# Summing attention values over slots: two strided reductions a tile instead of pairwise additions

## The chip, the cores and the metric

The kernel runs on one core of a Trainium2 chip. The time is that of one execution on the device, in microseconds (us). The engines have these names in the profile: PE is TensorE (matrix multiplications), PEld its weight loads, DVE is VectorE, ACT is ScalarE, POOL is GpSimd, SP is SyncE. Each engine works through its own instructions in order, and waits for the others through semaphores.

## The reference

The computation is a graph network on 6250 nodes with features of 128 numbers and some 206,000 edges. A first layer spreads features along the edges five times, and a layer norm follows. The second layer is an attention over the edges that arrive at a node:

```
q = (node_attr @ Wq).reshape(n, H, DQ // H)
k = conv(x[src], edge_attr, edge_sh, ..k).reshape(e, H, DK // H)
v = conv(x[src], edge_attr, edge_sh, ..v).reshape(e, H, DV // H)
alpha = einsum('ehq,qk,ehk->eh', q[dst], Wdot, k)
ealpha = exp(alpha - amax[dst])
attn = ealpha / denom[dst]
out = segment_sum(attn[..., None] * v, dst)
return out.reshape(n, DV) @ Wout
```

Here `conv` is `((x_src * (edge_sh @ Wang.T)) @ Wlin) * (relu(edge_attr @ W1 + b1) @ W2)`. There are H = 8 heads; a key has 64 numbers and a value 128, so 16 per head. A last layer norm follows. The change concerns the sum in `out`: for each node, its edges' weighted values are added up.

## The kernel before

The kernel has three stages: it counts edges between nodes in matrices (to about 600 us), it multiplies features with these matrices five times (to about 2140 us), and then comes the attention (`attend`, L859 to L1121), to the end. The first two stages aren't touched.

For the attention, nodes are sorted by their number of edges and put in 49 tiles of 128 nodes, one node per partition. Tile t has `WIDTHS[t]` slots, from 64 to 22, and 1658 in all; a slot holds one edge of every node of the tile. Four slots make a group (the last group of a tile may have fewer), and the loop at L1097 goes over the groups of all tiles as one pipeline, a few groups deep. For a group:

- `fetch` (L914), three groups ahead: POOL issues one indirect DMA per slot (L932), which gathers the features of the edges' source nodes into `xs`, of which there are six buffers.
- `turn` (L956): PE transposes `xs` into PSUM (L961), ACT copies it to `xT` (L964).
- `nets` (L966): PE computes `p_h` and `p_g` from the edge features (L975), ACT applies relu (L977), and DVE multiplies `p_g` with `xT` into `mkv` by two operations (L983). `p_g` has one buffer, so PE's next `nets` waits for this.
- `radial` (L987), one group later: PE computes `p_r` (L994), ACT copies it to `rr` (L998).
- `keys` (L1000): PE computes keys and values in `p_k` (L1008, L1010); `p_k` has one buffer. DVE multiplies them with `rr` into `kv` (L1015), which also frees `p_k`, and then forms the scores `al` (L1017, L1019).

When all groups of a tile are done, `softmax(t)` (L1022) is started. It is a generator, and it goes on to its next `yield` whenever the loop calls `step(running)`: once after `nets` of a group and once after `radial` and `turn` (L1103 and L1108), so twice a group, beside the groups of the next tile. The order of PE, DVE and ACT is this order of the program (`manual_schedule`, L1096). POOL's gathers stand in its own queue in the order of `fetch`.

The steps of `softmax` are: (1) mask, maximum and difference of the scores (L1030 to L1032); (2) exp on ACT (L1034); (3) mask again, denominator, reciprocal (L1036 to L1040); then, for each eight slots, a multiplication of the values with the weights in place (L1046), and from the second eight on an addition onto the first eight (L1050), each a step of its own; then one step with three additions of 4, 2 and 1 slots (L1053); then the division `o` (L1057), a transpose on PE (L1060) and the output product, the residual and the statistics (L1065 to L1067). After tiles 13, 26, 39, 46, 48 and 49 the finished rows are normalised (L1077) and POOL scatters them to the output (L1081), one indirect DMA per tile.

`kv` of a tile is an array of [128, w, 192] floats: per slot 64 numbers of the key and behind them 128 of the value. Neighbouring slots are thus 192 x 4 = 768 bytes apart. Two such arrays exist, used by turns.

Of the kernel before, what the change touches and what calls it, by code (L numbers as in the profile page):

```python
# [7 lines left out]
F32 = mybir.dt.float32  # L8
# [5 lines left out]
OP = mybir.AluOpType  # L14
AX = mybir.AxisListType
# [3 lines left out]
P = 128  # L19
# [12 lines left out]
H = 8  # L32
DK = 64
D = 128
# [174 lines left out]
def stats(nc, work, z, v):  # L209
    st = work.tile([P, nc.vector.BN_STATS_DIM], F32, name="st")  # L210
    nc.vector.bn_stats(st, z)
    nc.vector.bn_aggr(v, st)
# [646 lines left out]
def attend(tc, w1, b1, wang, w2, wlin, wqd, wout, ident, rows, c_iota, src_all, eas_o, x1_d, x1_r, out):  # L859


    nc = tc.nc
    WM = WIDTHS[0]
    with ExitStack() as s:
        one = s.enter_context(tc.tile_pool(name="at1", bufs=1))
        two = s.enter_context(tc.tile_pool(name="at2", bufs=2))
# [12 lines left out]
        with tc.tile_pool(name="at_w", bufs=1) as pool:  # L879
            wz = pool.tile([P, 2 * D], F32, name="wz")  # L880
            nc.vector.memset(wz, 0.0)
            for src, dst, at in ((w1, w1_s, 0), (wang, wang_s, 64)):
                n = src.shape[1]
                nc.vector.tensor_copy(dst, wz[:, :n])
                w = pool.tile([16, n], F32, name=f"w_{at}")
# [20 lines left out]
        def ps(name):  # L906
            return pp.tile([P, CH], F32, name=name, tag="ps")
# [114 lines left out]
        def softmax(t):  # L1022

            w = WIDTHS[t]
            a = kv[t]
            l = al.pop(t)[:, :w]
            ex = two.tile([P, WM, H], F32, name="ex")
            m = two.tile([P, H], F32, name="m")
            d = two.tile([P, H], F32, name="d")
            nc.vector.tensor_tensor(l, l, keep[t][:, :w, None].to_broadcast([P, w, H]), OP.min)  # L1030
            nc.vector.tensor_reduce(m, l.rearrange("p j h -> p h j"), AX.X, OP.max)
            nc.vector.tensor_tensor(l, l, m[:, None, :].to_broadcast([P, w, H]), OP.subtract)  # L1032
            yield
            nc.scalar.activation(ex[:, :w], l, AF.Exp)  # L1034
            yield
            nc.vector.tensor_tensor(ex[:, :w], ex[:, :w],  # L1036
                                    ok[t][:, :w, None].to_broadcast([P, w, H]), OP.mult)
            nc.vector.tensor_reduce(d, ex[:, :w].rearrange("p j h -> p h j"), AX.X, OP.add)
            nc.vector.tensor_scalar(d, d, none[:, t:t + 1], None, OP.add)
            nc.vector.reciprocal(d, d)  # L1040
            yield

            for u in range(0, w, 8):
                k = min(8, w - u)
                av = a[:, u:u + k, DK:].rearrange("p j (h f) -> p j h f", h=H)
                nc.vector.tensor_tensor(av, av, ex[:, u:u + k, :, None].to_broadcast([P, k, H, D // H]),  # L1046
                                        OP.mult)
                yield
                if u > 0:
                    nc.vector.tensor_add(a[:, :k, DK:], a[:, :k, DK:], a[:, u:u + k, DK:])  # L1050
                    yield
            for h in (4, 2, 1):
                nc.vector.tensor_add(a[:, :h, DK:], a[:, :h, DK:], a[:, h:2 * h, DK:])  # L1053
            yield
            av = a[:, :1, DK:].rearrange("p j (h f) -> p j h f", h=H)
            o = two.tile([P, H, D // H], F32, name="o")
            nc.vector.tensor_tensor(o, av[:, 0], d[:, :, None].to_broadcast([P, H, D // H]), OP.mult)  # L1057
            yield
            tr = ps("tr4")
            nc.tensor.transpose(tr[:, :P], o.rearrange("p h d -> p (h d)"), ident)  # L1060
            oT = two.tile([P, P], F32, name="oT")
            nc.scalar.copy(oT, tr[:, :P])
            yield
            y = ps("y4")
            nc.tensor.matmul(y[:, :D], oT, wo, start=True, stop=True)  # L1065
            nc.vector.tensor_add(z[:, t, :], x1s.pop(t), y[:, :D])
            stats(nc, two, z[:, t, :], v[:, t, :])  # L1067
            if t + 1 in NORMS:
                yield
                t0 = NORMS[NORMS.index(t + 1) - 1]  # L1070
                rs = two.tile([P, NT], F32, name="rs")
                n = t + 1 - t0
                nc.vector.tensor_scalar(rs[:, :n], v[:, t0:t + 1, 1], EPS, None, OP.add)
                nc.scalar.activation(rs[:, :n], rs[:, :n], AF.Sqrt)
                nc.vector.reciprocal(rs[:, :n], rs[:, :n])
                for u in range(t0, t + 1):
                    nc.vector.tensor_scalar(z[:, u, :], z[:, u, :], v[:, u, 0:1],  # L1077
                                            rs[:, u - t0:u - t0 + 1], OP.subtract, OP.mult)

                    k = min(P, N - u * P)  # L1080
                    st = nc.gpsimd.indirect_dma_start(  # L1081
                        out=out[:, :], in_=z[:k, u, :], in_offset=None,
                        out_offset=bass.IndirectOffsetOnAxis(ap=rows[:k, u, 0:1], axis=0)).ins
                    for q in puts:
                        tc.declare_no_dep(st, q, reason="a node has one place in the order")
                    puts.append(st)
                    if u % 4 == 3:
                        yield
# [7 lines left out]
        with tc.manual_schedule(engines=MANUAL):  # L1096
            for i in range(-3, len(groups) + 1):  # L1097
                live = [0 <= i + x < len(groups) for x in range(-1, 4)]
                if live[4]:
                    fetch(i + 3)  # L1100
                if live[1]:
                    nets(i)
                step(running)  # L1103
                if live[0]:
                    radial(i - 1)
                if live[2]:
                    turn(i + 1)
                step(running)  # L1108
                if live[0]:
                    keys(i - 1)  # L1110
                    t, j, n = groups[i - 1]
                    if j + n == WIDTHS[t]:
                        running.append(softmax(t))
                if len(running) > 1:
                    step(running)
                if live[3] and groups[i + 2][1] == 0:
                    begun.append(begin(groups[i + 2][0]))
                step(begun)
            for r in running:
                for _ in r:  # L1120
                    pass  # L1121
# [351 lines left out]
```

## Time and profile before

| | us |
|---|---|
| median of 10 runs | 4434.86 (4428.51 to 4440.15) |
| the profiled execution | 4440.44 |
| its span, first to last instruction | 4438.7 |
| first to last gather of the attention (L932) | 2142.8 to 4385.8 |
| DVE busy, whole span | 3615.9 |
| PE busy, whole span | 3721.4 |
| POOL busy, whole span | 2437.9 |

In a row of a group of instructions stand its line, engine, operation, written and read tiles with their shapes (partitions x elements), the number of instructions, their busy time in us, the mean of one in ns, and the idle time of the engine just before them with what ended it. A row on one line's instructions gives the shortest, median and longest duration in ns and the first and last start. A row of a timeline gives the start, the length, the engine and line, and in brackets the idle time before it and what ended that.

### The profile page before, as it was taken

The numbers are of one execution on the slowest core, as the hardware profiler recorded it, in microseconds if no ns is written. First come the engines' busy times: TensorE is split into PE (matmuls) and PEld (weight loads), VectorE is DVE, ScalarE is ACT, GpSimd is POOL, SyncE is SP. The second block draws the span as 40 slices with busy tenths as digits, with TensorE's granted clock in tenths as the row PEclk, the third lists the DMA queues.
The fourth block names the chain that finished last, engine by engine and source line by source line (L and its number), as shares of the span: only waits on it lengthen the run. The fifth ranks groups of instructions, "written<-read, shape, count | busy, mean of one in ns | idle before, by whom it ended". The sixth has DMA issues, their size and how long they took to land.

```text
span 4438.7 us, 70265 instructions
## 1 busy us (share of the span) xinstructions
PE 3721.4 (84%) x23256; PEld 3306.8 (75%) x23256; DVE 3615.9 (81%) x6081; ACT 2060.2 (46%) x4185; POOL 2437.9 (55%) x2388
## 2 busy tenths in 40 slices
PE   2555569979999999999588998878898878888885
PEld 2555558868888888887587888868888778887785
DVE  4999978657777878665488888879888978899796
ACT  1666665445564665643243433434443434344343
POOL 4233100653333443022677777777777777777774
PEclk9667679989999999999899999989999999999997
DMA  3555345668777888654555555545555655555541
GB/s 109 156 160 161 86 124 141 161 174 236 232 225 219 235 241 239 185 159 132 110 98 101 100 99 106 100 95 103 100 100 96 112 98 99 99 100 103 98 98 44
DMA packets 393183, 603.04 MB, mean 136 GB/s; under 512 B 122942, under 2 KB 328054, under 8 KB 381931
## 3 DMA queue, kind: packets, MB, share of 16 engines
q1 hardware_dynamic: 260352, 361.35, 33.2%
q0 software_dynamic: 128624, 207.89, 20.9%
q10 hardware_dynamic: 3834, 29.20, 2.1%
q8 instruction: 189, 3.10, 0.3%
q14 instruction: 184, 1.50, 0.1%
HBM read 493.45 MB, written 132.25 MB: 141 GB/s over the span
## 4 chain that ended last, share of the span: by engine, by line
PE 45%; DVE 16%; issue 11%; DMA 10%; POOL 10%; SPq 6%; ACT 1%; DVEq 0%; ACTq 0%; POOLq 0%
PE acc L588 23%; DMA xs<-x_d,src_all 7%; PE p_r L994 6%; POOL xs L932 6%; SPq L364 6%; PE p_k L1010 6%; PE p_k L1008 4%; DVE mkv L983 3%; DVE kv L1015 3%; PE p_g L975 2%; DVE oh_h L218 2%; PE p_x L961 2%; DVE oh_l L218 2%; DMA c<-counts 1%; POOL rows_d L747 1%
## 5 line engine op out<-in xcount | busy, mean ns | idle before, releaser
L932 POOL DMA_INDIRECT xs<-x_d,src_all x1658 | 1675.6, 1011 | 506.8 <-issue 432.1
L588 PE MATMUL acc<-c,parts 128*128 128x512 f32 (+1 forms) x6370 | 1412.6, 382 | 55.0 <-DVE c L571 40.7
L588 PEld LDWEIGHTS acc<-c,parts 128*128 128x128 f32 x6370 | 1155.4, 189 | 282.5 <-DVE c L571 47.1
L571 DVE CAST c<-c 128x1024 fp32r<-128x1024 uint8 x980 | 682.3, 714 | 258.0 <-PE acc L588 192.9
L1010 PE MATMUL p_k<-wlin_s,mkv 128*128 128x128 f32 x3316 | 760.2, 312 | 0.0
L584 ACT CAST c<-c 128x512 fp32r<-128x512 uint8 x735 | 454.9, 622 | 561.5 <-PE acc L588 430.8
L1008 PE MATMUL p_k<-wlin_s,mkv 128*128 128x64 f32 x3316 | 585.0, 260 | 65.2 <-DVE kv L1015 64.4
L994 PE MATMUL p_r<-w_s,r 128*128 128x192 f32 x3316 | 621.8, 330 | 0.0
L994 PEld LDWEIGHTS p_r<-w_s,r 128*128 128x128 f32 x3316 | 573.2, 194 | 34.8 <-ACT rr L998 0.2
L1008 PEld LDWEIGHTS p_k<-wlin_s,mkv 128*128 128x128 f32 x3316 | 528.0, 200 | 94.4 <-DVE kv L1015 93.3
L1015 DVE TENSOR_TENSOR kv<-rr,p_k 128x768 f32<-128x768 f32 (+2 forms) x443 | 396.7, 897 | 209.1 <-PE p_k L1010 192.6
L998 ACT COPY rr<-p_r 128x768 f32<-128x768 f32 (+2 forms) x443 | 334.8, 758 | 479.7 <-PE p_r L994 464.1
L983 DVE TENSOR_TENSOR mkv<-p_g,xT 128x512 f32<-128x512 f32 (+3 forms) x866 | 533.8, 658 | 6.6 <-PE p_g L975 6.5
L1010 PEld LDWEIGHTS p_k<-wlin_s,mkv 128*128 128x128 f32 x3316 | 527.8, 201 | 0.0
L977 ACT ACTIVATE r<-p_h,b_s 128x512 f32<-128x512 f32 (+3 forms) x433 | 289.8, 669 | 463.2 <-PE p_h L975 456.3
L812 POOL DMA_DIRECT2D eas_o<-eT_l x252 | 203.1, 809 | 507.8 <-DVE eT_l L806 499.7
L342 PE MATMUL p_c<-oh_h,oh_l 128*128 128x100 bf16 x3136 | 301.9, 273 | 169.4 <-DVE oh_h L218 168.4
L342 PEld LDWEIGHTS <-oh_l 128*128 128x128 bf16 x3136 | 290.3, 123 | 177.6 <-DVE oh_h L218 176.0
L961 PE MATMUL p_x<-ident,xs 128*128 128x128 f32 x1658 | 278.6, 280 | 128.2 <-DMA xs<-x_d,src_all 121.3
L961 PEld LDWEIGHTS p_x<-ident,xs 128*128 128x128 f32 x1658 | 212.8, 142 | 161.2 <-DMA xs<-x_d,src_all 127.8
L344 ACT CAST cT<-p_c 128x500 uint8<-128x500 f32 (+1 forms) x637 | 306.3, 638 | 47.1 <-DVE c_row L350 46.9
L964 ACT COPY xT<-p_x 128x512 f32<-128x512 f32 (+3 forms) x433 | 247.9, 573 | 136.1 <-PE p_x L961 132.0
(215 smaller groups left out, 4338.0 us busy)
## 6 DMA issues: line engine op xcount, KB each, us to landing
c<-counts SPq DMA_DIRECT2D x360, 384.0 KB
ea<-eas_o SPq DMA_DIRECT2D x648, 128.0 KB
c<-counts SPq DMA_DIRECT2D x120, 448.0 KB
eas_o<-eT_l POOLq DMA_DIRECT2D x162, 256.0 KB
counts<-c_row SPq DMA_DIRECT2D x582, 48.0 KB
xs<-x_d,src_all POOLq DMA_INDIRECT x1658
eat<-in_eas ACTq DMA_DIRECT2D x31, 832.0 KB
counts<-c_row SPq DMA_DIRECT2D x194, 56.0 KB
```

Of the source, the lines that this page charges most:

```text
L342: nc.tensor.matmul(p_c[:, q - q0], oh_los[t % 2][:, q // Q, :, q % Q], oh_hi[:, q // Q, :, q % Q], start=True, stop=True)
L571: nc.vector.tensor_copy(c[:, u:u + 1024].rearrange("p (n b x) -> p n b x", n=2, b=2), r[:, :, v:v + 512].rearrange("p b (n x) -> p n b x", ...
L584: nc.scalar.copy(c[:, 1024:w].rearrange("p (b x) -> p b x", b=2), r[:, :, 512:])
L588: nc.tensor.matmul(a[:, :v - u], parts[:, j, i, :], c[:, u:v], start=(j == 0 and i == 0), stop=(j == NT - 1 and i == 1))
L932: nc.gpsimd.indirect_dma_start(out=xs[g][:, i, :], out_offset=None, in_=x1_d[:, :], in_offset=bass.IndirectOffsetOnAxis(ap=src_all[:, c:c ...
L961: nc.tensor.transpose(p_x[:, i * P:(i + 1) * P], xs[g][:, i, :], ident)
L983: nc.vector.tensor_tensor(mkv[g][:, i, :n].rearrange("p j (b e) -> p b j e", b=4), p_g[:, i, :n * P].rearrange("p (b j e) -> p b j e", b=4 ...
L994: nc.tensor.matmul(p_r[:, i // 2, u:u + DK + D], r[:, i, :], w2_s, start=True, stop=True)
L998: nc.scalar.copy(r2[:, b, :f], p_r[:, b, :f])
L1008: nc.tensor.matmul(p_k[:, i // 2, u:u + DK], m[:, 0, i, :], wlin_s[:, :DK], start=True, stop=True)
L1010: nc.tensor.matmul(p_k[:, i // 2, u + DK:u + DK + D], m[:, 1, i, :], wlin_s[:, DK:], start=True, stop=True)
L1015: nc.vector.tensor_mul(k.rearrange("p (b i) f -> p b (i f)", b=b.stop - b.start), r2[:, b, :f], p_k[:, b, :f])
```

## The change

The multiplications stay as they are, one for each eight slots and each a step. The additions between them and the three additions behind them go. In their place come two reductions with an addition, one for the first four heads and one for the other four, each a step. One reduction reads, for each of 64 value columns, the w slots of the tile, and writes 64 sums into a new small tile `s`. The division then reads `s`.

```diff
                 nc.vector.tensor_tensor(av, av, ex[:, u:u + k, :, None].to_broadcast([P, k, H, D // H]),
                                         OP.mult)
                 yield
-                if u > 0:
-                    nc.vector.tensor_add(a[:, :k, DK:], a[:, :k, DK:], a[:, u:u + k, DK:])
-                    yield
-            for h in (4, 2, 1):
-                nc.vector.tensor_add(a[:, :h, DK:], a[:, :h, DK:], a[:, h:2 * h, DK:])
-            yield
-            av = a[:, :1, DK:].rearrange("p j (h f) -> p j h f", h=H)
+            s = two.tile([P, H, D // H], F32, name="s")
+            for h in range(0, H, 4):
+                f = DK + h * (D // H)
+                nc.vector.tensor_reduce(s[:, h:h + 4].rearrange("p h f -> p (h f)"),
+                                        a[:, :w, f:f + D // 2].rearrange("p j f -> p f j"), AX.X, OP.add)
+                yield
             o = two.tile([P, H, D // H], F32, name="o")
-            nc.vector.tensor_tensor(o, av[:, 0], d[:, :, None].to_broadcast([P, H, D // H]), OP.mult)
+            nc.vector.tensor_tensor(o, s, d[:, :, None].to_broadcast([P, H, D // H]), OP.mult)
```

## The prediction
> **What bounds the kernel now.** I read the page, then the groups of VectorE (DVE) from 2130 us on (the attention stage), the rows of single lines, and one tile's timeline.
>
> ```profile
> span 4438.7 us, 70265 instructions
> ...
> L932 POOL DMA_INDIRECT xs<-x_d,src_all x1658 | 1675.6, 1011 | 506.8 <-issue 432.1
> ```
> ```profile
> L932 POOL DMA_INDIRECT xs<-x_d,src_all x1658: 948/955/2015, 2142.8 to 4385.8; - x185
> ```
> The gathers alone set the pace of this stage: 1675.6 + 506.8 = 2182 us, plus about 65 us of output scatters, fill the 2243 us between the first and the last gather. POOL's idle time is "issue", about 0.3 us a gather. But its lead over DVE and TensorE (PE) is small:
>
> ```profile
> PE p_x L961 <- DMA xs<-x_d,src_all: 121.3, 80, 8.3
> PE p_k L1008 <- DVE kv L1015: 62.2, 98, 1.7
> PE tr L1060 <- DVE o L1057: 43.2, 43, 2.9
> ```
> These are PE's waits in the stage (total, times, longest). Only 121 of 2243 us are waits for gathers: DVE and PE would need some 2120 us without them. Next, what the change touches:
>
> ```profile
> L1050 DVE TENSOR_TENSOR kv<-kv 128x1024 f32<-128x1024 f32 (+7 forms) x180 | 197.2, 1096 | 5.9
> L1053 DVE TENSOR_TENSOR kv<-kv 128x512 f32<-128x512 f32 x147 | 68.8, 468 | 3.5
> ```
> ```profile
> L1031 DVE TENSOR_REDUCE m<-al x49: 470/645/1126, 2247.0 to 4408.2; 128x8 f32<-128x272 f32 x4, 128x8 f32<-128x296 f32 x3, 128x8 f32<-128x288 f32 x3, 128x8 f32<-128x280 f32 x3
> ...
> L1347 DVE TENSOR_REDUCE nviol<-viol x1: 1831/1831/1831, 25.5 to 25.5; 128x1 f32<-128x1612 f32 x1
> ```
> And how the work interlocks, in a tile of 36 slots:
>
> ```profile
> 3007.16 1.28 DVE L983 TENSOR_TENSOR mkv<-p_g,xT 128x512 f32<-128x512 f32 x2
> 3008.36 1.22 DVE L1046 TENSOR_TENSOR kv<-kv,ex 128x1024 f32<-128x1024 f32 x1
> 3009.61 1.22 DVE L1050 TENSOR_TENSOR kv<-kv 128x1024 f32<-128x1024 f32 x1
> 3010.75 0.95 DVE L1015 TENSOR_TENSOR kv<-rr,p_k 128x768 f32<-128x768 f32 x1
> 3011.75 0.43 PE L1008 MATMUL p_k<-wlin_s,mkv 128*128 128x64 f32 x2 [0.72 <-DVE kv L1015]
> 3012.53 1.28 DVE L983 TENSOR_TENSOR mkv<-p_g,xT 128x512 f32<-128x512 f32 x2
> ...
> 3028.74 1.47 DVE L1053 TENSOR_TENSOR kv<-kv 128x512 f32<-128x512 f32 x3
> 3030.24 0.29 DVE L1057 TENSOR_TENSOR o<-kv,d 128x128 f32<-128x128 f32 x1
> 3030.68 0.30 PE L1060 MATMUL tr<-ident,o 128*128 128x128 f32 x1 [0.98 <-DVE o L1057]
> ```
> A group of four slots costs DVE 2.97 us without softmax work (5.36 between starts of mkv, less the two operations' 2.39). PE needs 4.22 us a group (in the light groups p_h at L975 starts at 3040.13 and 3044.34). So softmax work beyond 1.25 us in a group makes DVE the limit, and PE then waits at the p_k bank that L1015 frees.
>
> **The change, part by part.** *Removed:* 180 additions (L1050) and 147 (L1053): 197.2 + 68.8 = 266 us of DVE.
>
> *Added:* 98 reductions of 64 x w elements (w slots in the tile, 1658 in all). Each output value is read along slots, 768 bytes apart. The trace has no such stride; two rows bound it. Contiguous (L1347): 1831 ns for 1612 elements, and L1019's 420 against 220 ns for 256 against 64: 1.04 ns an element. At a step of 32 bytes (L1031: 470 ns at w = 22, 176 elements; 1126 ns at w = 64, 512 elements): 656 / 336 = 1.95 ns an element and 0.126 us fixed. Both are the same operation, so the step between reads makes the difference, and I take 1.95, the scattered one being nearer. 2 x 64 x 1658 = 212,224 elements give 414 us, and 98 x 0.126 us give 12: 426 us. Net: +160 us of DVE. At 1.04 it is 221 + 12 = 233: net -33. Upward no row limits it; a step as large again would add another (1.95 - 1.04) x 212 = 193 us.
>
> The Trainium skill ("VectorE: DVE Perf Modes", section on the perf-mode tier table) puts tensor_reduce at one element a cycle whatever the type. At its 0.96 GHz that is 221 us, as with the contiguous row, and by it the change would save DVE time. The row L1031 says otherwise for scattered reads, and the sum goes by the row.
>
> *Where it lies.* A reduction of the 36-slot tile is one DVE instruction of 64 x 36 x 1.95 + 126 = 4.62 us. Behind it on DVE's queue stand L1015, which frees p_k for PE, and the next mkv, which frees p_g. Softmax steps come two to a group; the first reduction is step 4 + ceil(w/8). With ceil(w/8) odd (w of 33 to 40, and 24 and 22: 23 tiles) both fall into one group, with it even they fall into neighbouring groups (26 tiles).
>
> The 36-slot tile before, between starts of mkv: 5.72, 5.37, 5.36, 5.36, 4.30, 5.28, 5.00, 4.43, 4.55 = 45.4 us. After: 5.72 (unchanged); 5.36 (two multiplications); 2.97 + 1.22 + 0.68 = 4.9 (the last two); 2.97 + 2 x 4.62 + 0.1 = 12.3 (both reductions); then PE's transpose stands before its keys and waits for o, so DVE does mkv and o (1.6), waits 1.9 for the keys, and does the rest (1.8): 5.3; then 4.6, 4.4, 4.3, 4.55. Sum 51.4: +6 us, of which 3.5 is added DVE work and the rest is that early groups were freed of additions they could partly hide. I take 5.8 at the class's mean width of 34.7: 23 x 5.8 = 133.
>
> Split case, w = 30 (a reduction is 3.87 us): the groups 5.57 (mask, denominator, a multiplication), 5.36, 5.36, 2.97 + 2 x 0.95 = 4.87, 4.9 (the three additions, o), 5.0 (transpose) = 31.1 become 5.57, 5.36, 2.97 + 0.95 + 3.87 = 7.8, 2.97 + 3.87 + 0.29 = 7.1, 4.6 (transpose), 4.3 = 34.8. That is +3.7; the DVE work alone is +2.9, and as PE still has one group ahead at the first reduction I take +3: 20 x 3 = 60. Five tiles of 41 to 46 slots, with reductions of 5.2 to 5.9 us, at 4.5, and the 64-slot tile, with 8.1 us, at 10: 32. Together 133 + 60 + 32 = +225 us for DVE and PE.
>
> *What hides part of it.* The gathers go on during a reduction; six buffers of xs let POOL run ahead. So PE's 121 us of waits for gathers go first: 225 - 121 = +104. No more can hide, since POOL's pace no longer decides.
>
> *What comes back.* PE will stand still for up to 10 us a tile (both reductions, L1015, mkv, o, less what it has ahead). The trace shows the price of idling:
>
> ```profile
> 3579.80 0.45 PE L961 MATMUL p_x<-ident,xs 128*128 128x128 f32 x1 [8.25 <-DMA xs<-x_d,src_all]
> ```
> ```profile
> 3575.00:3588.70 13.70, 6.80 (x26) 5.66 (x27) 2.41 (x5) 1.36 (x3) 10.35 (x12) 0.50 0.18 48
> 3588.70:3598.00 9.30, 8.36 (x62) 7.68 (x61) 5.93 (x15) 3.65 (x7) 7.17 (x8) 1.00 0.31 80
> ```
> (The second view: stretch, length, busy time of PE, its weight loads, DVE, ACT and POOL, then granted clock, DMA share, GB/s.) After 8.25 us of idling the granted clock (0.50, then 1.00) is half for some 9 us of resumed work; after idle stretches of 2 us (as at 3103.65) it is half for 3.4 or 6.8 us (the trace's record of the clock). Each reduction stall will cost such a stretch: 1.7 to 3.4 us of PE time while PE is the limit. I take the low end, as some lies beside DVE work: 49 x 1.7 = 83.
>
> *Gathers.* Their mean is 1011 ns against a least of 948, so contention costs at most 0.063 x 1658 = 104 us, and the additions are about a third of the time of DVE's operations with two operands in SBUF (266 of some 760 us, L1046 with 253 and L1017 with 180 the others): some 35 us of POOL time. The Trainium skill ("SBUF — State Buffer", section on who interferes with whom) says that such an operation blocks a GpSimd instruction reading SBUF, and a reduction never does. By it the change would free POOL, which no run here shows. Those 35 us are worth nothing once POOL does not set the pace, so I take 0.
>
> Sum: 225 - 121 + 83 = +187 us on the profiled execution's 4440.44 us, which stands 5.6 us above the median 4434.86: 4434.9 + 187 = 4622 us.
>
> **The rivals.** *A, POOL still hides it.* The stalls would have to fit into what gathers run ahead. For: POOL never shows a wait for a buffer over 0.3 us, and PE mostly reaches a tile's first gather 7 to 18 us after its issue (by the timeline). Against: a buffer moves a stall, and the 36-slot tile's 51.4 us exceeds POOL's 46. Time 4430 to 4480; it needs a sum of 150 us or less where I have 225.
> *B, faster.* If the 768-byte step is read at 1.04 ns an element, a reduction takes 2.5 us, DVE loses 33 us of work, POOL stays the limit, and fewer two-operand operations shorten gathers by up to 35 us: 4400 to 4430. It decides below about 1.1 ns. Against it stands L1031.
> *C, dearer reads.* If 768 bytes costs a step more than 32 bytes, another 193 us, hidden by nothing: some 4820.
>
> **How the numbers follow.** My case 0.74 (own range 4530 to 4780: from no clock loss at 4434.9 + 104 to about half of the waits kept with the clock at 3.4 us), A 0.09, B 0.08, C 0.09. The range runs 4450 to 4790: my case with its bounds and most of A. This kernel can be told from no change at about 0.2% (9 us). Faster 0.08 (B), same 0.04 (half of A), slower 0.88.
>
> **What would show it.** Two reductions a tile near 4.3 us at w = 34, 426 us in all; DVE's idle time lower; PE's wait at L1008 for L1015 in stretches of several us; the wait for xs nearly gone, and gathers waiting over 0.3 us for p_x; half-clock stretches at each tile. It is wrong if a reduction takes 2.4 us (then B), if PE's stalls stay below 3 us a tile (then A), or if the half clock does not follow them (then some 4540).

## The result, and the profile after

The changed kernel takes 4651.2 us (median of 8; 4645.7 to 4655.7) where the kernel before took 4435.0 us (median of 28): a ratio of 1.0486, with a 95% interval of 1.0477 to 1.0495. That is 216 us slower; 187 were forecast. First the head of the page, of the kernel before and then of the changed kernel (busy time, share of the span and number of instructions of each engine):

```profile
PE 3721.4 (84%) x23256; PEld 3306.8 (75%) x23256; DVE 3615.9 (81%) x6081; ACT 2060.2 (46%) x4185; POOL 2437.9 (55%) x2388
```
```profile
span 4648.9 us, 70024 instructions
...
PE 3805.5 (82%) x23256; PEld 3394.2 (73%) x23256; DVE 3723.1 (80%) x5852; ACT 2060.5 (44%) x4185; POOL 2401.7 (52%) x2388
...
L932 POOL DMA_INDIRECT xs<-x_d,src_all x1658 | 1640.3, 989 | 732.2 <-issue 435.0 <-PE p_x L961 245.3 <-DMA xs<-x_d,src_all 19.9
```
PE's line keeps the books of the whole change. It has the same 23256 instructions, but is busy for 84 us more: it ran more of them at half clock (the mean granted clock of the whole run fell from 0.926 to 0.892). And it is idle for 4648.9 - 3805.5 = 843 us in place of 4438.7 - 3721.4 = 717: 126 us more. Both together are the 210 us by which the span grew. POOL, which before waited for PE's L961 to free a buffer of xs for 20 us in all and never over 0.3 us at a time, now waits 245 us for it, up to 9.1 us at a time: its gathers no longer set the pace.

Next, what PE waited for from the start of the attention stage to the end of the kernel (total us, times, longest), in the kernel before and then in the changed kernel:

```profile
PE p_x L961 <- DMA xs<-x_d,src_all: 121.3, 80, 8.3
PE p_k L1008 <- DVE kv L1015: 64.4, 99, 2.1
PE tr L1060 <- DVE o L1057: 57.0, 45, 12.3
PE y L1065 <- ACT xT L964: 38.9, 43, 0.9
```
```profile
PE tr L1059 <- DVE o L1056: 257.9, 49, 14.5
PE p_k L1008 <- DVE kv L1015: 119.6, 110, 6.5
...
PE y L1064 <- ACT xT L964: 19.5, 25, 0.9
...
PE p_x L961 <- DMA xs<-x_d,src_all: 7.7, 8, 2.5
```
So the waits for DVE grew by 256 us, those for gathers fell by 114, and those of the product y by 19: +123 of the 126 us. The longest wait for o, 14.5 us, is that of the last tile, and was 12.3 before.

The reductions, by form, and one tile of 36 slots in the order of time:

```profile
L1052 DVE TENSOR_REDUCE s<-kv 128x64 f32<-128x1408 f32 x2 | 4.9, 2500 | 0.0
...
L1052 DVE TENSOR_REDUCE s<-kv 128x64 f32<-128x2304 f32 x6 | 24.1, 4053 | 0.0
...
L1052 DVE TENSOR_REDUCE s<-kv 128x64 f32<-128x4096 f32 x2 | 14.1, 7052 | 0.0
```
```profile
3087.38 0.33 PE L1008 MATMUL p_k<-wlin_s,mkv 128*128 128x64 f32 x2
...
3087.61 1.28 DVE L983 TENSOR_TENSOR mkv<-p_g,xT 128x512 f32<-128x512 f32 x2
3088.80 8.03 DVE L1052 TENSOR_REDUCE s<-kv 128x64 f32<-128x2304 f32 x2
3096.75 0.94 DVE L1015 TENSOR_TENSOR kv<-rr,p_k 128x768 f32<-128x768 f32 x1
...
3099.78 0.28 DVE L1056 TENSOR_TENSOR o<-s,d 128x128 f32<-128x128 f32 x1
...
3100.20 0.45 PE L1059 MATMUL tr<-ident,o 128*128 128x128 f32 x1 [8.73 <-DVE o L1056]
...
3100.44 0.53 PE L1008 MATMUL p_k<-wlin_s,mkv 128*128 128x64 f32 x2
...
3104.17 0.95 DVE L1015 TENSOR_TENSOR kv<-rr,p_k 128x768 f32<-128x768 f32 x1 [4.12 <-PE p_k L1010]
```
The two reductions hold DVE for 8 us. Behind them stand L1015, the next group's mkv and o, and PE's transpose waits for that o: 8.73 us without work. PE then comes back at half clock (0.53 us for the pair at L1008, in place of 0.33 ahead of the stall), and DVE in turn waits 4.12 us for the keys. At full clock it would still wait some 2.3 us, as `warm2` below shows.

### The profile page after: what moved, and what is told of

Same layout as the page of the kernel before. It is cut to its first block, busy times and chain, and to the rows that moved or that the text cites. A ratio compares the mean times of both kernels' runs of the same rounds, so it can differ in the third digit from the quotient of the medians.

```text
span 4648.9 us, 70024 instructions
## 1 busy us (share of the span) xinstructions
PE 3805.5 (82%) x23256; PEld 3394.2 (73%) x23256; DVE 3723.1 (80%) x5852; ACT 2060.5 (44%) x4185; POOL 2401.7 (52%) x2388
## 4 chain that ended last, share of the span: by engine, by line
PE 43%; DVE 29%; issue 14%; SPq 5%; POOL 4%; DMA 2%; ACT 1%; ACTq 0%; DVEq 0%; POOLq 0%
PE acc L588 23%; DVE mkv L983 7%; PE p_r L994 6%; PE p_k L1010 5%; SPq L364 5%; DVE kv L1015 5%; DVE s L1052 4%; PE p_k L1008 3%; DVE kv L1046 3%; DVE kv L1017 2%; DVE oh_h L218 2%; PE p_g L975 2%; PE p_x L961 2%; DVE oh_l L218 2%; POOL rows_d L747 1%
## 5 line engine op out<-in xcount | busy, mean ns | idle before, releaser
L932 POOL DMA_INDIRECT xs<-x_d,src_all x1658 | 1640.3, 989 | 732.2 <-issue 435.0
L1010 PE MATMUL p_k<-wlin_s,mkv 128*128 128x128 f32 x3316 | 791.5, 323 | 0.0
L1008 PE MATMUL p_k<-wlin_s,mkv 128*128 128x64 f32 x3316 | 607.3, 268 | 121.6 <-DVE kv L1015 119.6
L1008 PEld LDWEIGHTS p_k<-wlin_s,mkv 128*128 128x128 f32 x3316 | 551.2, 209 | 156.2 <-DVE kv L1015 155.9
L994 PE MATMUL p_r<-w_s,r 128*128 128x192 f32 x3316 | 648.8, 340 | 0.0
L1015 DVE TENSOR_TENSOR kv<-rr,p_k 128x768 f32<-128x768 f32 (+2 forms) x443 | 396.7, 897 | 298.9 <-PE p_k L1010 255.1
L994 PEld LDWEIGHTS p_r<-w_s,r 128*128 128x128 f32 x3316 | 594.7, 201 | 31.1 <-ACT rr L998 0.2
L1010 PEld LDWEIGHTS p_k<-wlin_s,mkv 128*128 128x128 f32 x3316 | 552.9, 209 | 0.0
L1052 DVE TENSOR_REDUCE s<-kv 128x64 f32<-128x2176 f32 (+22 forms) x98 | 373.0, 3826 | 0.9
L975 PE MATMUL p_g<-ea,wang_s 128*128 128x512 f32 (+3 forms) x866 | 294.6, 423 | 14.9 <-DVE mkv L983 14.2
L961 PE MATMUL p_x<-ident,xs 128*128 128x128 f32 x1658 | 263.6, 280 | 22.6 <-DVE z L1065 8.1
```

Source lines behind the costliest of these rows:

```text
L932: nc.gpsimd.indirect_dma_start(out=xs[g][:, i, :], out_offset=None, in_=x1_d[:, :], in_offset=bass.IndirectOffsetOnAxis(ap=src_all[:, c:c ...
L975: nc.tensor.matmul(o[:, :n * P], wt, e, start=True, stop=True)
L994: nc.tensor.matmul(p_r[:, i // 2, u:u + DK + D], r[:, i, :], w2_s, start=True, stop=True)
L1008: nc.tensor.matmul(p_k[:, i // 2, u:u + DK], m[:, 0, i, :], wlin_s[:, :DK], start=True, stop=True)
L1010: nc.tensor.matmul(p_k[:, i // 2, u + DK:u + DK + D], m[:, 1, i, :], wlin_s[:, DK:], start=True, stop=True)
L1015: nc.vector.tensor_mul(k.rearrange("p (b i) f -> p b (i f)", b=b.stop - b.start), r2[:, b, :f], p_k[:, b, :f])
```

## The experiments

Two theories were set against each other. Theory 1, that of the prediction: the cost lies in where the reductions stand, two long ones together ahead of what PE needs, and in the half clock that follows the stall. Theory 2: it is the added amount of DVE work (373 us of reductions for 266 us of additions, +107 us), wherever it stands. Unless said otherwise, each edit is made to the changed kernel, whose ratio to the kernel before is 1.0486. All ratios are to the kernel before, on the same chip. The changed kernel itself was not run beside these edits. Where the text says how many us an edit saves against it, the two times come from different sessions, whose kernels before differ by 2 to 5 us; worked out from the ratios, the savings are 5 to 11 us smaller.

**Four runs that could not be read as times.** The kernels `apart`, `late`, `p4` and `flat`, described below, ran first on a chip on which the attention stage stalled in all engines, with idle time put down to "issue" and "remote" that the other traces don't have. The kernel before took 4967 us there. From the waits of `flat`:

```profile
DVE kv L1015 <- remote: 325.8, 70, 15.7
ACT r L977 <- remote: 286.6, 52, 10.0
```
They gave 1.0166 (1.0116 to 1.0215), 1.0146 (1.0095 to 1.0197), 1.0195 (1.0141 to 1.0249) and 1.0106 (1.0055 to 1.0157). The changed kernel itself did not run there, so they say nothing on the theories, except by the durations of the reductions, which are those of the later runs (2.34 us in the median in `flat`). The expectations were:

> One more empty step ahead of the first reduction in the 23 tiles where both reductions fell into one group, so that in every tile they fall into neighbouring groups, with one L1015 and one mkv between them. Same DVE work as the changed kernel. Theory 1 (what costs is that the two reductions stand together in DVE's queue and PE runs dry for 8 to 9.5 us at the transpose that waits for o): these stalls become two of some 3 us, about 2.5 to 3 us of stall less a tile and 1 us or so less of half clock, 23 x 4 = 90 us: 4560 us (4530 to 4600). Theory 2 (the amount of DVE work alone costs: 373 us of reductions in place of 266 us of additions): nothing moves, 4651 us within 10.

> Two more empty steps between the division o and PE's transpose, in every tile; DVE's order is unchanged, PE's transpose moves one group later. Theory 1: PE's wait for o (237 us in the changed kernel) goes, and PE waits at the keys (L1008) for L1015 instead, which ends 2.3 us earlier (mkv 1.2, L1017 and L1019 0.8, o 0.3): 49 x 1 to 2.3 us less, 4540 to 4600 us. Theory 2 (amount of DVE work): 4651 us within 10.

> Four reductions of 32 columns a tile in place of two of 64, each a step: the same elements, about 2.1 us each at 34 slots, and 98 more instructions with a fixed part of about 0.25 us, 25 us more of DVE. Theory 1 (concentration): no group holds more than 4.3 us of reductions, PE's longest waits fall from 9 to about 4 us, half-clock stretches get fewer: 4470 to 4560 us. Theory 2 (amount): 4651 + 25 = 4676 us.

> The two reductions read as many elements into as many outputs, in the same places of the order, but from neighbouring addresses; what they add up is not the weighted values by head, so the sum over slots is left out as such. If the step of 768 bytes is what makes a reduction cost 1.65 ns an element, a reduction falls to 1.04 ns an element, 2.5 us at 34 slots and 235 us in all, and the time to that of my rival B: 4400 to 4440 us, with POOL's gathers the limit again. If a long reduction is dear in itself, durations stay near 3.8 us and the time at 4651 us.

All four were run again on two other chips, where the kernel before took 4433 us (`late2`, `p4b`, `flat2`, and `warm`) and 4430 us (`apart2` and the rest).

**The transpose two steps later (`late2`).**

```diff
             nc.vector.tensor_tensor(o, s, d[:, :, None].to_broadcast([P, H, D // H]), OP.mult)
             yield
+            yield
+            yield
             tr = ps("tr4")
```


> The same kernel as late, once more, for the same reason. Theory 1: PE's wait for o goes and becomes a shorter one at L1008 for L1015: 1 to 2.3 us a tile less than the changed kernel, 4540 to 4600 us. Theory 2 (amount of DVE work): 4651 us within 10.

Measured: 4571.2 us, 1.0324 (1.0307 to 1.0341), 80 us less than the changed kernel with the same DVE work (3723.8 us busy). The same tile as above:

```profile
3072.14 8.03 DVE L1052 TENSOR_REDUCE s<-kv 128x64 f32<-128x2304 f32 x2
3080.09 0.94 DVE L1015 TENSOR_TENSOR kv<-rr,p_k 128x768 f32<-128x768 f32 x1
...
3081.09 0.69 PE L1008 MATMUL p_k<-wlin_s,mkv 128*128 128x64 f32 x2 [6.28 <-DVE kv L1015]
```
PE's stall is 6.28 us in place of 8.73: it ends with L1015 and no longer with o. That is 2.45 us less, where 2.3 were worked out. Theory 2 falls here as the whole account: the time moved by 80 us with DVE's work unchanged. It isn't excluded as a part. Of the 140 us by which this run is still slower than the kernel before, no run tells how much is the added DVE work itself.

**Four reductions of 32 columns (`p4b`).**

```diff
-            for h in range(0, H, 4):
+            for h in range(0, H, 2):
                 f = DK + h * (D // H)
-                nc.vector.tensor_reduce(s[:, h:h + 4].rearrange("p h f -> p (h f)"),
-                                        a[:, :w, f:f + D // 2].rearrange("p j f -> p f j"), AX.X, OP.add)
+                nc.vector.tensor_reduce(s[:, h:h + 2].rearrange("p h f -> p (h f)"),
+                                        a[:, :w, f:f + 2 * D // H].rearrange("p j f -> p f j"), AX.X, OP.add)
                 yield
```


> The same kernel as p4, once more, for the same reason. Theory 1 (concentration): 4470 to 4560 us, with PE's longest waits in the stage near 4 us in place of 9. Theory 2 (amount of DVE work): 4676 us.

Measured: 4553.6 us, 1.0276 (1.0258 to 1.0293): 98 us less, though the reductions take 387 us in place of 373 (25 us more were expected, 14 were measured). PE's waits for DVE, and the stalls in the tile of 36 slots:

```profile
PE p_k L1008 <- DVE kv L1015: 182.0, 162, 3.3
PE tr L1059 <- DVE o L1056: 124.8, 45, 13.6
```
```profile
3070.56 0.43 PE L1008 MATMUL p_k<-wlin_s,mkv 128*128 128x64 f32 x2 [2.42 <-DVE kv L1015]
...
3080.10 0.30 PE L1059 MATMUL tr<-ident,o 128*128 128x128 f32 x1 [3.44 <-DVE o L1056]
```
That is 307 us in place of 378, and two stalls of 2.4 and 3.4 us stand where one of 8.7 stood. More DVE work in smaller pieces is faster, as theory 1 says.

**Both reductions in neighbouring groups in every tile (`apart2`).**

```diff
             s = two.tile([P, H, D // H], F32, name="s")
+            if -(-w // 8) % 2:
+                yield
             for h in range(0, H, 4):
```


> The same kernel as apart, once more, as that run was disturbed on its chip. Theory 1: the 23 stalls of 8 to 9.5 us become two of some 3 us each: 23 x 4 = 90 us less than the changed kernel, 4560 us (4530 to 4600). Theory 2 (amount of DVE work): 4651 us.

Measured: 4604.5 us, 1.0405 (1.0385 to 1.0425): 47 us less where 90 were expected, just outside the expected 4530 to 4600. PE's waits for DVE fell by 82 us, to 167.8 + 127.8 us. But its busy time didn't fall with them (3821.7 against 3805.5 us). The tile of 36 slots:

```profile
3080.55 0.43 PE L1008 MATMUL p_k<-wlin_s,mkv 128*128 128x64 f32 x2 [2.38 <-DVE kv L1015]
...
3081.19 0.53 PE L1008 MATMUL p_k<-wlin_s,mkv 128*128 128x64 f32 x2
...
3087.06 0.30 PE L1061 MATMUL tr<-ident,o 128*128 128x128 f32 x1 [2.14 <-DVE o L1058]
...
3091.51 0.53 PE L1008 MATMUL p_k<-wlin_s,mkv 128*128 128x64 f32 x2
```
Two stalls of 2.4 and 2.1 us, shorter than the 3 us expected, brought the half clock as the one of 8.7 did. The mean granted clock of the stage from 2400 to 4350 us is 0.90, against 0.89 in the changed kernel and 0.96 in the kernel before. The direction is theory 1's; the expectation had the clock recover with shorter stalls, which it did not. In `p4b` the mean is 0.94, with stalls that in this tile are no shorter but stand 9.5 us apart instead of 6.5; whether the distance makes the difference was not tried.

**PE kept busy during the wait (`warm`, `warm2`).** Filler matmuls go into unused columns of the transpose's bank; their results are not read.

```diff
             tr = ps("tr4")
+            if -(-w // 8) % 2:
+                for _ in range(w):                  # warm2: w + 7 * w // 10
+                    nc.tensor.matmul(tr[:, P:3 * P], w1_s, wang_s, start=True, stop=True)
             nc.tensor.transpose(tr[:, :P], o.rearrange("p h d -> p (h d)"), ident)
```


> The changed kernel with one filler matmul per slot (128 x 256, into unused columns of the transpose's bank) ahead of PE's transpose, in the 23 tiles where both reductions share a group. They fill some 6 of the 8 to 9.5 us for which PE waits for o there; the wait itself stays. If the half clock after the stalls costs 3 us a tile, as the keys' 0.86 us a pair in place of 0.45 suggest, the time falls by 23 x 2 to 3 us, to 4580 to 4610 us, and the half-clock stretches (505 us of the stage in the changed kernel) shrink to some 250. If the half clock costs nothing, 4651 us or, where the fillers overrun the wait, more.

`warm`: 4644.6 us, 1.0489 (1.0471 to 1.0506), as the changed kernel. The fillers were too few:

```profile
3091.72 4.58 PE L1061 MATMUL tr<-wang_s,w_s 128*128 128x256 f32 x36 [0.94 <-ACT xT L964]
3099.67 0.33 PE L1062 MATMUL tr<-ident,o 128*128 128x128 f32 x1 [3.37 <-DVE o L1056]
...
3100.79 0.53 PE L1008 MATMUL p_k<-wlin_s,mkv 128*128 128x64 f32 x2
```
PE stood idle for 3.37 us at the end of the wait, and about 1 us after it the matmuls are at half speed again. So this run could not tell.

> As warm, with 1.7 filler matmuls a slot in place of one. In warm the fillers ended 3.4 us before the wait did, and the half clock came all the same, 1 us after the wait's end; here they last the whole wait (61 x 0.127 = 7.8 us of some 8 us at 36 slots). If the half clock after the stalls costs up to 3 us a tile, the time falls by 23 x 2 to 3 us, to 4580 to 4610 us; if it costs nothing, it stays at 4640 to 4655 us.

`warm2`: 4610.6 us, 1.0414 (1.0396 to 1.0431), 41 us less than the changed kernel by the times and 32 by the ratios; its interval and that of the changed kernel don't overlap. DVE's order is unchanged, and PE's transpose still has to wait until o is done; most of that wait is now filled with matmuls (71 us of idle time are left of 258). In the tile that was shown (here the wait ends at 3087.21):

```profile
3087.21 0.33 PE L1062 MATMUL tr<-ident,o 128*128 128x128 f32 x1 [0.37 <-DVE o L1056]
3087.38 0.33 PE L1008 MATMUL p_k<-wlin_s,mkv 128*128 128x64 f32 x2
```
The keys behind the wait run at full clock. 32 to 41 us in the 23 tiles with fillers are 1.4 to 1.8 us a tile for the half clock.

**The price of the stride alone (`flat2`).** The reductions read neighbouring addresses; their sum is of other numbers, as the expectation of `flat` says.

```diff
-                f = DK + h * (D // H)
+                f = h // 4 * 64 * w
                 nc.vector.tensor_reduce(s[:, h:h + 4].rearrange("p h f -> p (h f)"),
-                                        a[:, :w, f:f + D // 2].rearrange("p j f -> p f j"), AX.X, OP.add)
+                                        a.rearrange("p j c -> p (j c)")[:, f:f + 64 * w].rearrange(
+                                            "p (f j) -> p f j", j=w), AX.X, OP.add)
```


> The same kernel as flat, once more, since in that run's attention stage the engines also stood still on issue and on waits put down to remote, the kernel before (4967 us there) too. There the reductions took 2.34 us in the median, as contiguous reads should. Expected without those: 4400 to 4440 us, POOL's gathers the limit again (rival B). If it stays more than 1% above the kernel before here too, the order of the softmax steps costs by itself, whatever the reads cost.

Measured: 4465.0 us, 1.0086 (1.0069 to 1.0103). Its tile of 36 slots:

```profile
3081.99 5.00 DVE L1052 TENSOR_REDUCE s<-kv 128x64 f32<-128x2304 f32 x2
3086.91 0.94 DVE L1015 TENSOR_TENSOR kv<-rr,p_k 128x768 f32<-128x768 f32 x1
3089.88 0.28 DVE L1057 TENSOR_TENSOR o<-s,d 128x128 f32<-128x128 f32 x1
...
3090.30 0.45 PE L1060 MATMUL tr<-ident,o 128*128 128x128 f32 x1 [5.65 <-DVE o L1057]
```
PE's waits for DVE:

```profile
PE tr L1060 <- DVE o L1057: 185.1, 49, 12.6
PE p_k L1008 <- DVE kv L1015: 81.3, 110, 3.8
```
The stride is what makes the reductions dear: they take 233 us in all in place of 373, 2.5 us in place of 4.05 for this tile. DVE has less work than in the kernel before (3580.2 us busy against 3615.9), and yet the kernel is 32 us slower, against the expectation of 4400 to 4440: PE still waits 185 us for o and 81 us for L1015. The 0.9% are less than the 1% that the expectation set as a sign that the order of the steps costs by itself, but the whole interval lies above 1. So of the 216 us some 180 go with the stride (the longer reductions, and the stalls and half clock that they bring), and 32 remain with short reads. PE is busy for as long as in the kernel before (3721.3 against 3721.4 us): these 32 us are waiting.

**A version that might beat both (`turnedl`).**

```diff
-            for u in range(0, w, 8):
-                k = min(8, w - u)
-                av = a[:, u:u + k, DK:].rearrange("p j (h f) -> p j h f", h=H)
-                nc.vector.tensor_tensor(av, av, ex[:, u:u + k, :, None].to_broadcast([P, k, H, D // H]),
-                                        OP.mult)
-                yield
             s = two.tile([P, H, D // H], F32, name="s")
             for h in range(0, H, 4):
                 f = DK + h * (D // H)
+                for u in range(0, w, 16):
+                    k = min(16, w - u)
+                    av = a[:, u:u + k, f:f + D // 2].rearrange("p j (h f) -> p j h f", h=4)
+                    e = ex[:, u:u + k, h:h + 4, None].to_broadcast([P, k, 4, D // H])
+                    to = av if w > WP else prod[:, :, :, u:u + k].rearrange("p h f j -> p j h f")
+                    nc.vector.tensor_tensor(to, av, e, OP.mult)
+                    yield
                 nc.vector.tensor_reduce(s[:, h:h + 4].rearrange("p h f -> p (h f)"),
-                                        a[:, :w, f:f + D // 2].rearrange("p j f -> p f j"), AX.X, OP.add)
+                                        a[:, :w, f:f + D // 2].rearrange("p j f -> p f j") if w > WP else
+                                        prod[:, :, :, :w].rearrange("p h f j -> p (h f) j"), AX.X, OP.add)
                 yield
```
with `prod` a tile of [128, 4, 16, 46] floats and `WP` 46, and the two steps of `late2` ahead of the transpose.

> A version that might beat both: the multiplications go over four heads and 16 slots and write their products turned into a small tile of its own, slots side by side, so that the two reductions read neighbouring addresses; one reduction follows each half's multiplications, so they stand some 4 steps apart; and the transpose comes two steps after o. The tile of 64 slots keeps strided reads. Reductions: 1.04 ns an element, 235 us in all. Open is what a write with a step of 184 bytes costs: if nothing, the multiplications stay at 1.2 us, DVE has 31 us less work than before, nothing stands together, and POOL's gathers set the pace with fewer additions in their way: 4390 to 4430 us. If a scattered write costs 1.65 ns an element as the scattered read does, the multiplications grow by 0.6 us each, 110 us in all: 4440 to 4520 us.

Measured: 4520.6 us, 1.0209 (1.0192 to 1.0226). The second case of the expectation, at the upper end of its 4440 to 4520: scattered writes are about as dear as scattered reads. A row of a window of the stage, and the gathers:

```profile
L1053 DVE TENSOR_TENSOR prod<-kv,ex 128x1024 f32<-128x1024 f32 x114 | 223.5, 1968 | 0.8
```
```profile
L934 POOL DMA_INDIRECT xs<-x_d,src_all x1658 | 1755.5, 1059 | 507.9 <-issue 434.9 <-DMA xs<-x_d,src_all 28.3 <-PE p_x L963 12.5
```
A multiplication of 1024 elements takes 1.97 us in place of 1.21 (1.21 us also in this run, in the tile of 64 slots, which writes in place). DVE is as busy as in the changed kernel (3733.1 against 3723.1 us), and with reductions and multiplications spread over the steps and the transpose later the kernel is 131 us faster than that. What then sets the pace is POOL again: it hardly waits for a buffer (12.5 us), and its gathers have grown to 1059 ns in the mean. With the idle time ahead of them they take 1755.5 + 507.9 = 2263 us, 81 more than in the kernel before, and the whole kernel takes 90 us more. No version was found that beats the kernel before.

**Does POOL set the pace before? (`beforelate1`)** To the kernel before:

```diff
             nc.vector.tensor_tensor(o, av[:, 0], d[:, :, None].to_broadcast([P, H, D // H]), OP.mult)
             yield
+            yield
             tr = ps("tr4")
```


> The kernel before with one empty step between o and the transpose. PE waits 43 us for o there. If POOL's gathers set the pace of the stage, as the prediction says, this changes nothing: within 10 us of the kernel before. If DVE and PE set it, 20 to 45 us faster.

Part of this kernel's output differs from that of the kernel before, for a reason that was not traced; its engines execute as many instructions (6081 on DVE, 23256 on PE), so the time is that of the same work. Measured: 4431.1 us, 1.0001 (0.9991 to 1.0011). PE's wait for o fell to 24.9 us, and one of 49.9 us at L961 for DVE's z came in its place; the wait for gathers stayed (108.7 us). This agrees with the gathers setting the pace, but as the waits moved rather than went, it shows less than was meant.

## Why the prediction was right

*What bounds the kernel before.* Held: the gathers, with a lead that lasts no longer than PE's 121 us of waits for them. Those went to 7.7 us, and POOL began to wait for buffers.

*The removed and added work.* The additions' 266 us are as read. The reductions take 373 us, not 426: from w = 22 (1408 elements, 2500 ns) to w = 64 (4096 elements, 7052 ns) it is 1.69 ns an element, and 1.65 between w = 34 and 36, where the row with a step of 32 bytes gave 1.95. The row was the right one of the two (`flat2` has the other, 1.04, with 233 us in all, the number that was worked out for it), but it is 15% too dear for a step of 768 bytes. The Trainium skill's one element a cycle ("VectorE: DVE Perf Modes", the section on the perf-mode tier table) holds for `flat2`, and not for the changed kernel. Net +107 us of DVE where +160 was said.

*Where it lies.* The parity of the steps holds: 23 tiles with one stall for o, of 6.2 to 9.5 us but for the last tile, and shorter ones at L1008 in the others. So the wait that grew is mostly the one for o (+201 us); the wait at L1008, which was named as the sign to look for, grew by 55. The sum for DVE and PE, +225 us, compares with 256 - 19 = 237 us of added waits. That it came out close although a reduction is 12% shorter means that something else costs more than I counted. The tile of 36 slots shows where. Its nine groups, between starts of mkv, take 53.3 us, against 45.4 before: 7.9 us more, where 6 were said and 1.7 for the clock. In `warm2`, with the clock kept up, they take 51.5 us, where 51.4 were said, though the two reductions take 8.3 us there and not 9.2. The two groups with the reductions and the transpose take 11.2 + 5.5 us (12.3 + 5.3 were said); the group behind them takes 6.5 in both runs, where 4.6 were said. In the changed kernel:

```profile
3110.13 0.95 DVE L1015 TENSOR_TENSOR kv<-rr,p_k 128x768 f32<-128x768 f32 x1 [2.15 <-PE p_q L947]
```
PE comes out of its stall behind DVE, and DVE still waits for it a group later. This part of the stall I left out; the reductions, priced too dear, made up for it, which is luck.

*What hides part of it.* 121 us were said to go, 114 went.

*What comes back.* 83 us for the half clock. PE's busy time grew by 84 us, and `warm2` gives 1.4 to 1.8 us a tile where the fillers are, near the 1.7 that was taken. That both agree so well is partly luck: 84 us of PE's work need not all lie on the path, and `warm2` says nothing of the 26 other tiles. Together, 237 - 114 + 84 = 207 of the measured 216 us, where 225 - 121 + 83 = 187 were said.

*Gathers.* Their mean fell from 1011 to 989 ns, which is 36 us of POOL (35 were said), and it was worth nothing, as said. That a reduction does not hold up a gather, which was open, shows in the tile of 36 slots: the seven gathers that POOL issues while its two reductions run take 0.95 to 0.96 us each.

*The rivals.* A needed a sum of 150 us or less; it was 237. C, a read dearer than the 32-byte step, is excluded by 1.65. B is excluded for the changed kernel by the price of a read, but its own price was wrong: `flat2` has B's reads, and at 4465 us it isn't faster than the kernel before. The mechanism of the stall works at 2.5 us a reduction too, which I left out there.

## What to carry to other kernels

A reduction over scattered addresses is priced by its reads (1.65 to 1.95 ns an element here, 1.04 from neighbouring addresses): look for a row with scattered reads, and count scattered writes in the same way. A long instruction on an engine that two others wait for costs more than its duration: read what is queued behind it, find out who runs dry and for how long, and add what the idle time does to TensorE's clock. Stalls need not be long for that: those of `apart2` last 2.1 and 2.4 us in the tile shown. The same work in smaller pieces, or with its consumer a step later, can be worth more than less work.

## What was not expected of the hardware

The step of 32 bytes (L1031: 1.95 ns an element) is dearer than that of 768 bytes (1.65). Why was not tried.

A scattered write costs about as much as a scattered read: 1968 ns for 1024 elements with a step of 184 bytes, 1205 ns without, or 0.75 ns an element more, where the reads with a step of 768 bytes cost 0.65 more.

A gather that POOL issues while DVE runs an operation with two operands in SBUF ends only after it, if it begins well before its end. In the kernel before:

```profile
3013.72 1.21 DVE L1046 TENSOR_TENSOR kv<-kv,ex 128x1024 f32<-128x1024 f32 x1
...
3014.55 1.21 POOL L932 DMA_INDIRECT xs<-x_d,src_all  x1 [0.30 <-issue]
...
3186.98 1.17 DVE L1046 TENSOR_TENSOR kv<-kv,ex 128x1024 f32<-128x1024 f32 x1
...
3187.06 1.92 POOL L932 DMA_INDIRECT xs<-x_d,src_all  x1 [0.30 <-issue]
```
Both gathers end 0.83 us after the multiplication does, though one began 0.83 us into it and the other 0.08, and they take 1.21 and 1.92 us in place of 0.95. This fits what the Trainium skill says in "SBUF — State Buffer", section on who interferes with whom, of a DVE instruction with two inputs in SBUF and a GpSimd instruction that reads SBUF; a gather takes its row numbers from `src_all`, which lies there. In `turnedl`, whose multiplications last 1.97 us, a gather takes 1059 ns in the mean.

A stall of PE of 3.4 us (`warm`) was followed by half clock, about 1 us after its end, and stalls of 2.1 and 2.4 us (`apart2`) as well.
